# A graph layer on one core: the first gather of each part waits for ScalarE's work on the part three in front

## The chip, the cores and the metric

The kernel runs on one core of one Trainium2 chip. A core has a matrix engine (TensorE, written PE; its weight loads PEld), VectorE (DVE), ScalarE (ACT), GpSimd (POOL) and SyncE (SP, which here only issues transfers). Times are device microseconds (us) of one execution. The time before is the median of three runs.

## The reference

Nodes carry 128 features (`x`, 12,500 rows). There are 412,500 edges, sorted by their target node `dst`; each names a source node `src`.

```python
theta = x[dst] - x[src]
w = sigmoid(relu(theta @ W1 + b1) @ W2 + b2)
agg = segment_sum(w * theta, dst)
indeg = segment_sum(ones, dst)
y = x + agg + indeg * (x @ W4 + b4)
out = (y - mean(y)) / sqrt(var(y) + 1e-5)     # per row
```

## The kernel before

**Tables and parts.** The kernel first writes a table `z` to memory: for each node its row of `x @ W1` beside its row of `x`. The edges are then taken in 276 parts, numbered 0 to 275 (`s` in the code). Parts 0 to 17 are plain parts of 1,024 edges in the order given; parts 18 to 275 hold 1,532 edges each, of which 512 have one of the "hot" source nodes, whose rows TensorE makes from a table in on-chip memory (`tabs`), and at most 1,024 are gathered. Two parts make a block, which shares one sum in an accumulator.

**Gathers.** `gather(s)` issues eight indirect transfers from POOL (L401), each of 128 rows of 1 KB of `z`, into one of five buffers `zbuf` (`NZ = 5`); the last part has four. Part `s` uses the buffer of part `s - 5`. Since a gather overwrites a buffer, the framework makes it wait until its last readers are done: VectorE for the left half of the rows, ScalarE for the right half. It also waits for the landing of the gather eight before it (the counters `DMASW0` to `DMASW7`, one for each of the eight). POOL has next to nothing else to do in parts 18 to 275, and its gathers stand in the order of the parts.

**One part on the other engines.** `logits(s)` on VectorE subtracts the gathered rows from what TensorE spread over the edges (L951), applies the relu and the weights (L956), and sums (L962). ScalarE's `gate_sums` takes the sigmoid (L975), and `weigh_rest(s)` writes eight copies of the gathered rows, each weighted (L993, `wx`). L993 is the last reader of the part's buffer. TensorE adds the weighted copies up (L1158). Beside this VectorE works through `place()`, a long list of small steps that sorts the edges of the next 64 parts; `spend` hands them out by a credit per part. The sets of 64 begin at parts 18, 82, 146 and 210, and the gathers of a set need the indices that `place()` has made for it.

**What sets the order.** In the main loop (`part(s)`, for `s` from 18) the orders of TensorE, VectorE and ScalarE are as the code is written. POOL's gathers follow each other as they are issued. `gather` knows of a table `paced`: if the part is in it, the part's first gather gets one more wait, for the instruction noted there. In the kernel before, nothing is put into `paced`, so that the gathers are held back by the five buffers alone. `weighed[0]` always holds the newest weighted copy that was issued.

Gathers are issued four parts ahead in the early parts (`AHEAD = 4`) and three ahead in the main loop, from part 22 on, inside `spread_ahead`.

Of the kernel before, what the change touches and what calls it, by code (L numbers as in the profile page):

```python
# [37 lines left out]
AHEAD = 4  # L38
# [5 lines left out]
PLAIN = FIRST + MORE  # L44
# [40 lines left out]
def gnn_resnorm(  # L85
# [41 lines left out]
    NS = PLAIN - (E1 - E) // CE  # L127
# [32 lines left out]
    def set_of(s):  # L160

        s0 = 0 if s < PLAIN else PLAIN + (s - PLAIN) // S2 * S2
        return placed[s0], s - s0
# [8 lines left out]
    def load(i):  # L172

        s0, n, full = sets[i]
        es = ep.tile([P, WL], I32, name="es")
        ed = ep.tile([P, WL], I32, name="ed")
        bb = ep.tile([P, 1], I32, name="bb")
        dp = ep.tile([P, 1], I32, name="dp")
        e0 = E1 + (s0 - PLAIN) * CE
        if full < S2:  # L180
            nc.vector.memset(es, 0)
            for t in (ed, bb, dp):
                nc.vector.memset(t, N)
        for t, edges, m in ((es, src, HL), (ed, dst, WL)):
            for h in range(LISTS):
                nc.sync.dma_start(t[h * S2:h * S2 + full, :m], bass.AP(
                    tensor=edges.tensor, offset=edges.offset + e0 + h * HL, ap=[[CE, full], [1, m]]))
            if full < n:
                nc.sync.dma_start(
                    t[full:n, :TAIL], edges[E - TAIL:E].rearrange("(s e) -> s e", s=1))  # L190
        with nc.allow_non_contiguous_dma(reason="each block's and each part's first dst"):
            for h in range(LISTS):
                at = slice(h * S2, h * S2 + n)
                nc.sync.dma_start(bb[at], bass.AP(
                    tensor=dst.tensor, offset=dst.offset + e0, ap=[[SUB * CE, n // SUB], [0, SUB], [1, 1]]))
                nc.sync.dma_start(dp[at], bass.AP(
                    tensor=dst.tensor, offset=dst.offset + e0, ap=[[CE, n], [1, 1]]))
        return es, ed, bb, dp
# [172 lines left out]
    def slots(s):  # L371
        return [h * J + j for h in range(2) for j in range(pairs(s))]
# [7 lines left out]
    def wx_of(s):  # L380

        if s < NH:
            return wxe_buf[s % 2]
        return wx_buf[s % NW]

    def rows_of(s):

        if s < NH:
            t = zbuf[s // 2].rearrange("p k d -> p (k d)")[:, (s % 2) * BE:(s % 2 + 1) * BE]
            return t.rearrange("p (k d) -> p k d", d=D)  # L390
        return zbuf[(s - NH + NX) % NZ]
# [3 lines left out]
    paced = {}  # L395

    def gather(s):

        (src_i, _, _), i = set_of(s)
        for k in slots(s):  # L400
            ins = nc.gpsimd.indirect_dma_start(  # L401
                out=rows_of(s)[:, k, :], out_offset=None, in_=z if s >= NH else x,
                in_offset=IndirectOffsetOnAxis(ap=src_i[:, k, i:i + 1], axis=0))
            waits = [(gathers[-1], mybir.DependencyClass.NoSync)] if gathers else []
            at = (s * K + k) * 4 * len(chunks) // (NH * K) - 6
            if s < NH and 0 <= at < len(table_steps):
                waits.append((table_steps[at], mybir.DependencyClass.Sync))
            if k == 0 and s in paced:
                waits.append((paced[s], mybir.DependencyClass.Sync))
            for other, kind in waits:  # L410
                tc.add_manual_dep(
                    ins.ins, other.ins.name,
                    mybir.DependencyInfo(kind, mybir.DependencyReason.DATA), reason="gathers' pace")
            gathers.append(ins)
# [304 lines left out]
    with tc.manual_schedule(engines={SP}), tc.tile_pool(name="work", bufs=2) as wp, tc.tile_pool(  # L719
# [162 lines left out]
        def spread_y(s):  # L882

            d = parts[s]
            d["y"] = []
            for k0 in range(0, K if s < PLAIN else J, J):
                if s < NH:
                    spread_x(s, k0, copy_x(turn_x(s, k0)))
                    continue
                y = y_tile() if s < PLAIN - 1 else ps_y.tile([P, G, D], F32, name="y")  # L890
                d["y"].append(y)
                for j in range(J if s < PLAIN else pairs(s)):
                    nc.tensor.matmul(y[:, j, :], d["oh"][:, (k0 + j) * P:(k0 + j + 1) * P],  # L893
                                     y_of(s), start=True, stop=True)
# [94 lines left out]
        def weigh_rest(s):  # L989

            wx = wx_of(s)
            for k in slots(s):
                weighed[0] = nc.scalar.activation(wx[:, k, :D], rows_of(s)[:, k, D:], AF.Copy,  # L993
                                                  scale=wx[:, k, D:D + 1])
# [7 lines left out]
        weighed = [None]  # L1002
# [11 lines left out]
        def hot_load(f):  # L1014

            i0, g, i1, i = f
            a = i0
            while a < i1:
                (hot_s, _, n), j = hot_set(a)
                m = min(i1 - a, n - j)  # L1020
                nc.sync.dma_start(
                    hot_src[:, i % NU, (a - i0) * EP:(a - i0 + m) * EP],
                    hot_s[g, j:j + m].rearrange("(o p) l e -> o (p l e)", o=1).to_broadcast([P, m * EP]))
                a += m
# [77 lines left out]
        def hot_turned(t):  # L1102

            xT = xT_all[:, (t - PLAIN) % HX, :]
            nc.tensor.matmul(pz, wneg, xT, start=True, stop=False)  # L1105
            nc.tensor.matmul(pz, y_of(t), blocks[t // SUB]["oh"][:, BP:], start=False, stop=True)  # L1106

        def hot_relu(t):

            hr = parts[t]["hr"] = wp.tile([P, HK], F32, name="hr", bufs=1)  # L1110
            nc.scalar.activation(hr, pz, AF.Relu)  # L1111
# [169 lines left out]
        def fetch(b):  # L1281
            if b < NK:
                load_block(b)
# [48 lines left out]
        def tiles_of(group):  # L1332

            x = 0
            for f in group:
                hot_tiles(f, x)
                tiled.append((f, x))
                x += (f[2] - f[0]) * EP
# [19 lines left out]
        def fetch_step(s):  # L1358

            for f in rest_of:  # L1360
                if f[0] - 4 == s:
                    tiles_of([f])
# [125 lines left out]
        def spread_ahead(s):  # L1488

            if s + 2 < NS:  # L1490
                spread_y(s + 2)
                if PLAIN + AHEAD <= s + 3 < NS:
                    gather(s + 3)

        def part(s):

            b, h = divmod(s, SUB)
            t = s + 1
            credit[0] = min(credit[0] + 2.5, 5.0)
            if s in turns:  # L1500
                edges[s + 3] = turns[s], load(turns[s])
            if s in edges:
                i, loaded = edges.pop(s)
                assert steps[0] is None
                steps[:] = place(i, lambda: where[0](), *loaded), "k"
            for f in rest_of:
                if f[0] - 7 == s:
                    hot_load(f)
            if h == 0:
                fetch(b + 2)  # L1510
            if s == PLAIN:
                normalize(b - 2)
            done_b = h == 1 and PLAIN // SUB - 1 <= b - 1 < NK
            if t < NS:
                hot_turned(t)
            if t < NS:
                hot_relu(t)
            if done_b:
                total(b - 1)
            while opened:  # L1520
                hot_out(*opened.pop(0))
            advance("c")
            if s < NS:
                logits(s)
            if done_b:
                finish(b - 1)
            spread_ahead(s)
            if t < NS:
                hot_rows(t)
            sums = []  # L1530
            if h == 0 and PLAIN // SUB <= b - 1 < NK:
                sums = add_block(b - 1)
            if h == 1 and b < NK:
                sums = begin_block(b)
            issue(sums, products_of_tiles())
            if h == 0 and b + 1 < NK:
                one_hot(b + 1, BP, RW)
            if h == 1 and b + 2 < NK:
                one_hot(b + 2, 0, BP)
            if h == 1 and b < NK:  # L1540
                shift(b)
            if t < NS:
                hot_weights(t)
            if done_b:
                own(b - 1)
            if s < NS:
                if h == 0:
                    one_hot_h(b)
                gate_sums(s)
                weigh_rest(s)  # L1550
            fetch_step(s)
            spend("kxspmz")
            if done_b:
                normalize(b - 1)
# [204 lines left out]
```

## Time and profile before

| what | value |
|---|---|
| time, median of 3 runs | 2937.81 us (2935.55 to 2943.02) |
| the profiled execution's own time | 2943.8 us |
| its span, first to last instruction | 2942.0 us |
| busy: PE, PEld | 2548.2 us (87%), 2012.3 us (68%) |
| busy: DVE, ACT, POOL | 2380.3 us (81%), 2123.8 us (72%), 2164.5 us (74%) |
| gathers of parts 18 to 275 | 2060, 980 ns each in the mean |

A row of the timeline reads: start in us, duration in us, engine, line, operation, what is written `<-` what is read, how many instructions were merged, and in brackets how long the engine stood idle before it and what ended that. Rows of a source line begin with the line, the engine, the operation, the count, and the shortest, median and longest duration in ns. POOLq is POOL's sequencer. `zbuf<-z,src_i` as a DMA is a gather's landing. The first row of `zbuf<-z,src_i` is the first gather of part 18, so that a part's first gather is found by counting eights; in the same way the first L951 and the first eight L993 are those of part 18.

### The profile page before, as it was taken

What the parts mean: (1) busy time and instruction counts of PE and PEld (TensorE: products, weight loads), DVE (VectorE), ACT (ScalarE), POOL (GpSimd) and SP (SyncE); (2) the same over time, 40 slices, a digit from 0 to 9 for tenths busy, and PEclk for the clock granted to TensorE, in tenths of its full rate; (3) what the DMA queues carried; (4) which work ended last, traced back from release to release, by engine and by line L of the source; (5) the groups of instructions that cost most, each with busy time, mean ns of one, the idle gap of its engine ahead of it and who ended that gap; (6) DMA issues with size and microseconds to landing.
All of it is one profiled execution on the core that took longest, in us unless ns stands there. A gap on an engine that the chain in (4) does not pass through costs nothing.

```text
span 2942.0 us, 59129 instructions
## 1 busy us (share of the span) xinstructions
PE 2548.2 (87%) x18606; PEld 2012.3 (68%) x18606; DVE 2380.3 (81%) x4436; ACT 2123.8 (72%) x6416; POOL 2164.5 (74%) x2213
## 2 busy tenths in 40 slices
PE   6877899988888998998898888898998888888886
PEld 5656677777676777776776666676776666677764
DVE  7899699888957988888558888888568888888654
ACT  6365778767777777677777777776777777677776
POOL 4566777777777777777777777777777777777774
PEclk8688999989999999999999999999999999999998
DMA  8455555555554555554554545454554555555542
GB/s 285 151 153 123 142 139 138 140 135 137 140 146 134 137 140 140 133 141 135 143 150 133 135 133 141 132 141 134 143 142 128 140 132 141 133 138 141 141 134 77
DMA packets 239329, 413.58 MB, mean 141 GB/s; under 512 B 63423, under 2 KB 147226, under 8 KB 237470
## 3 DMA queue, kind: packets, MB, share of 16 engines
q0 software_dynamic: 105280, 286.93, 35.3%
q1 hardware_dynamic: 131756, 116.40, 15.3%
q10 hardware_dynamic: 1970, 6.40, 0.7%
q8 instruction: 148, 2.42, 0.3%
q14 instruction: 175, 1.43, 0.2%
HBM read 388.57 MB, written 20.94 MB: 139 GB/s over the span
## 4 chain that ended last, share of the span: by engine, by line
PE 38%; ACT 19%; DVE 15%; DMA 11%; issue 7%; POOL 1%; DVEq 0%; SPq 0%; ACTq 0%; POOLq 0%
PE pa L1158 14%; DMA zbuf<-z,src_i 10%; DVE zbuf L951 5%; PE y L893 5%; PE pd L1055 5%; ACT wx L993 5%; PE px L1119 4%; ACT wxh L1131 4%; PE pz L1105 3%; PE pz L1106 3%; PE pz L1122 3%; ACT oh L872 2%; ACT oh L873 2%; ACT xT L1069 1%; ACT a L1213 1%
## 5 line engine op out<-in xcount | busy, mean ns | idle before, releaser
L401 POOL DMA_INDIRECT zbuf<-z,src_i x2060 | 2018.5, 980 | 637.0 <-issue 236.6
L993 ACT ACTIVATE wx<-zbuf,wx 128x128 f32<-128x128 f32 x2060 | 630.2, 388 | 0.0
L1158 PE MATMUL pa<-wx,ow 128*104 128x260 f32 (+1 forms) x2284 | 628.4, 393 | 0.0
L893 PEld LDWEIGHTS y<-y,oh 128*128 128x128 f32 (+1 forms) x2156 | 276.1, 197 | 420.5 <-DVE zbuf L951 378.2
L1055 PEld LDWEIGHTS <-tabs 128*128 128x128 bf16 x6360 | 452.8, 101 | 124.2 <-issue 8.2
L951 DVE TENSOR_TENSOR zbuf<-y,zbuf 128x1024 f32<-128x1024 f32 x258 | 315.1, 1221 | 272.2 <-DMA zbuf<-z,src_i 270.9
L1055 PE MATMUL pd<-of,tabs 128*128 128x128 bf16 (+3 forms) x6360 | 535.2, 223 | 0.0
L1111 ACT ACTIVATE hr<-pz 128x512 f32<-128x512 f32 x258 | 152.9, 593 | 522.9 <-PE pz L1106 522.8
L893 PE MATMUL y<-y,oh 128*128 128x128 f32 (+1 forms) x2156 | 314.7, 291 | 228.7 <-DVE zbuf L951 220.6
L1158 PEld LDWEIGHTS pa<-wx,ow 128*104 128x104 f32 x2284 | 342.8, 179 | 40.6 <-issue 0.4
L962 DVE TENSOR_REDUCE lg<-zbuf 128x8 f32<-128x1024 f32 x273 | 329.8, 1208 | 13.2
L956 DVE SCALAR_TENSOR_TENSOR zbuf<-zbuf,fix 128x1024 f32<-128x1024 f32 x273 | 331.6, 1215 | 9.3
L1158 PE MATMUL pa<-wxh,owh 128*104 128x130 f32 x2064 | 329.0, 296 | 0.0
L1131 ACT ACTIVATE wxh<-pz,wxh 128x128 f32<-128x128 f32 x1032 | 295.2, 369 | 42.1 <-PE pz L1122 35.9
L1105 PE MATMUL pz<-xT,wni 128*128 128x512 f32 x516 | 278.5, 621 | 1.6 <-ACT wxh L1131 1.6
L1158 PEld LDWEIGHTS pa<-wxh,owh 128*104 128x104 f32 x2064 | 274.3, 186 | 0.0
L1119 PEld LDWEIGHTS px<-w_c,hr 128*128 128x128 f32 x2064 | 263.5, 200 | 7.8 <-ACT hr L1111 7.8
L1119 PE MATMUL px<-w_c,hr 128*128 128x1 f32 x2064 | 262.1, 248 | 5.6 <-ACT hr L1111 5.6
L1106 PE MATMUL pz<-oh,y 128*128 128x512 f32 x516 | 264.5, 594 | 0.1
L872 ACT ACTIVATE oh<-to_all,away,mine 128x512 f32<-128x512 bf16 (+1 forms) x257 | 213.6, 831 | 3.1 <-DMA to_all<-off_d 3.1
L1106 PEld LDWEIGHTS pz<-oh,y 128*128 128x128 f32 x516 | 98.2, 191 | 124.3 <-issue 123.4
L1122 PE MATMUL pz<-wni,xT 128*128 128x128 f32 x1032 | 176.3, 297 | 0.0
(304 smaller groups left out, 3595.8 us busy)
## 6 DMA issues: line engine op xcount, KB each, us to landing
to_all<-off_d SPq DMA_DIRECT2D x258, 128.0 KB
zbuf<-z,src_i POOLq DMA_INDIRECT x2060
hot_src<-hot_s SPq DMA_DIRECT2D x228, 128.0 KB
y<-z SPq DMA_DIRECT2D x270, 28.0 KB
xw<-in_x_dram SPq DMA_DIRECT2D x138, 52.0 KB
out_dram<-o SPq DMA_DIRECT2D x138, 52.0 KB
wx<-in_x_dram ACTq DMA_DIRECT2D x12, 512.0 KB
z<-zbuf SPq DMA_DIRECT2D x6, 1024.0 KB
```

What stands on the lines that cost most here:

```text
L401: ins = nc.gpsimd.indirect_dma_start(out=rows_of(s)[:, k, :], out_offset=None, in_=z if s >= NH else x, in_offset=IndirectOffsetOnAxis(ap= ...
L893: nc.tensor.matmul(y[:, j, :], d["oh"][:, (k0 + j) * P:(k0 + j + 1) * P], y_of(s), start=True, stop=True)
L951: nc.vector.tensor_sub(half, yy.to_broadcast([P, 2, n, D]), half)
L956: nc.vector.scalar_tensor_tensor(h[:, at, :], h[:, at, :], 0.0, w2.to_broadcast([P, n, D]), op0=OP.max, op1=OP.mult)
L962: nc.vector.tensor_reduce(lg[:, at, 0], h[:, at, :], AX.X, OP.add)
L993: weighed[0] = nc.scalar.activation(wx[:, k, :D], rows_of(s)[:, k, D:], AF.Copy, scale=wx[:, k, D:D + 1])
L1055: steps_of.append(lambda q=q, i=i, t=t, j=j: nc.tensor.matmul(to[:, q], tabs[:, g, i, q, t, :], of[:, t, q], start=j == 0, stop=j == HT * ...
L1105: nc.tensor.matmul(pz, wneg, xT, start=True, stop=False)
L1106: nc.tensor.matmul(pz, y_of(t), blocks[t // SUB]["oh"][:, BP:], start=False, stop=True)
L1119: nc.tensor.matmul(lgh()[:, t % SUB, q:q + 1], hr[:, at], w2_c, start=True, stop=True)
L1131: nc.scalar.activation(wx[:, q, :D], pz[:, q * P:(q + 1) * P], AF.Copy, scale=wx[:, q, D:D + 1])
L1158: return [lambda i=i, one=one, w=w: nc.tensor.matmul(to if len(w.shape) == 3 else to[:, 0, :], one, w, start=first and i == 0, stop=last a ...
```

## The change

Two lines leave `spread_ahead`, which stands in the first half of a part, and come back near the part's end, behind `weigh_rest(s)`. There the newest weighted copy, `weighed[0]`, is the eighth of part `s`; it is put into `paced[s + 3]` before `gather(s + 3)` is issued. So from part 22 on, the first of a part's eight gathers waits for the last weighted copy of the part three in front, besides the waits that it had.

```diff
@@ -1489,8 +1489,6 @@
             if s + 2 < NS:
                 spread_y(s + 2)
-                if PLAIN + AHEAD <= s + 3 < NS:
-                    gather(s + 3)
 
         def part(s):
@@ -1548,6 +1546,9 @@
                     one_hot_h(b)
                 gate_sums(s)
                 weigh_rest(s)
+            if PLAIN + AHEAD <= s + 3 < NS:
+                paced[s + 3] = weighed[0]
+                gather(s + 3)
             fetch_step(s)
             spend("kxspmz")
             if done_b:
```

On POOL, the last two gathers of part 25 and the eight of part 26 stand like this before. A row is one gather; the names with a number are the buffers and tables of this place, `Activation_49` and `DVE_49` are the counters of ScalarE and VectorE, and `DMASW` those of the landings. The value that is waited for is not shown.

```order
L401 DMA zbuf3_178<-z_60,src_i_2318 128x256 [waits DMASW6_49,Activation_49]
L401 DMA zbuf3_178<-z_60,src_i_2318 128x256 [waits DMASW7_49,Activation_49]
L401 DMA zbuf4_179<-z_60,src_i_2318 128x256 [waits DMASW0_49,DVE_49,Activation_49]
L401 DMA zbuf4_179<-z_60,src_i_2318 128x256 [waits DMASW1_49,Activation_49]
L401 DMA zbuf4_179<-z_60,src_i_2318 128x256 [waits DMASW2_49,Activation_49]
L401 DMA zbuf4_179<-z_60,src_i_2318 128x256 [waits DMASW3_49,Activation_49]
L401 DMA zbuf4_179<-z_60,src_i_2318 128x256 [waits DMASW4_49,Activation_49]
L401 DMA zbuf4_179<-z_60,src_i_2318 128x256 [waits DMASW5_49,Activation_49]
L401 DMA zbuf4_179<-z_60,src_i_2318 128x256 [waits DMASW6_49,Activation_49]
L401 DMA zbuf4_179<-z_60,src_i_2318 128x256 [waits DMASW7_49,Activation_49]
```

The same ten rows on POOL in the changed kernel:

```order
L401 DMA zbuf3_178<-z_60,src_i_2318 128x256 [waits DMASW6_49]
L401 DMA zbuf3_178<-z_60,src_i_2318 128x256 [waits DMASW7_49]
L401 DMA zbuf4_179<-z_60,src_i_2318 128x256 [waits DMASW0_49,DVE_49,Activation_49]
L401 DMA zbuf4_179<-z_60,src_i_2318 128x256 [waits DMASW1_49]
L401 DMA zbuf4_179<-z_60,src_i_2318 128x256 [waits DMASW2_49]
L401 DMA zbuf4_179<-z_60,src_i_2318 128x256 [waits DMASW3_49]
L401 DMA zbuf4_179<-z_60,src_i_2318 128x256 [waits DMASW4_49]
L401 DMA zbuf4_179<-z_60,src_i_2318 128x256 [waits DMASW5_49]
L401 DMA zbuf4_179<-z_60,src_i_2318 128x256 [waits DMASW6_49]
L401 DMA zbuf4_179<-z_60,src_i_2318 128x256 [waits DMASW7_49]
```

No gather has moved against another. The first of a part waits for a later value of ScalarE's counter, and the other seven no longer wait for ScalarE by themselves, since the first has done so for them.

The second place is POOL at the first part of the second set, part 82 (its table of indices is `src_i_8661`). Before:

```order
L401 DMA zbuf4_179<-z_60,src_i_2318 128x256 [waits DMASW6_49,Activation_49]
L401 DMA zbuf4_179<-z_60,src_i_2318 128x256 [waits DMASW7_49,Activation_49]
L401 DMA zbuf0_175<-z_60,src_i_8661 128x256 [waits DMASW0_49,DVE_49,Activation_49]
L401 DMA zbuf0_175<-z_60,src_i_8661 128x256 [waits DMASW1_49,Activation_49]
L401 DMA zbuf0_175<-z_60,src_i_8661 128x256 [waits DMASW2_49,Activation_49]
```

And in the changed kernel, on POOL:

```order
L401 DMA zbuf4_179<-z_60,src_i_2318 128x256 [waits DMASW6_49]
L401 DMA zbuf4_179<-z_60,src_i_2318 128x256 [waits DMASW7_49]
L401 DMA zbuf0_175<-z_60,src_i_8661 128x256 [waits DMASW0_49,DVE_49,Activation_49]
L401 DMA zbuf0_175<-z_60,src_i_8661 128x256 [waits DMASW1_49]
L401 DMA zbuf0_175<-z_60,src_i_8661 128x256 [waits DMASW2_49]
```

The new set's gathers follow the old set's at the same place of the row; only the waits differ. On TensorE, VectorE, ScalarE and SyncE every instruction stands where it stood, with the same kinds of waits.

## The prediction

> **What bounds the kernel now.** I read the page's busy shares first, then its groups, and then asked what POOL waits for.
>
> ```profile
> span 2942.0 us, 59129 instructions
> PE 2548.2 (87%) x18606; PEld 2012.3 (68%) x18606; DVE 2380.3 (81%) x4436; ACT 2123.8 (72%) x6416; POOL 2164.5 (74%) x2213
> L401 POOL DMA_INDIRECT zbuf<-z,src_i x2060 | 2018.5, 980 | 637.0 <-issue 236.6
> L951 DVE TENSOR_TENSOR zbuf<-y,zbuf 128x1024 f32<-128x1024 f32 x258 | 315.1, 1221 | 272.2 <-DMA zbuf<-z,src_i 270.9
> ```
>
> By busy shares TensorE leads and POOL comes fourth. But VectorE stands still 270.9 us for landings of gathers, and POOL's busy time leaves out what lies between two gathers. The waits of POOL from the first gather of part 22 to the end of part 274 (310.7 to 2910.7 us), and the gathers of that stretch:
>
> ```profile
> POOL zbuf L401 <- ACT wx L993: 142.7, 468, 0.3
> POOL zbuf L401 <- DMA zbuf<-z,src_i: 59.1, 194, 0.3
> ...
> L401 POOL DMA_INDIRECT zbuf<-z,src_i x2024: 942/949/1957, 310.7 to 2909.5; - x184
> ```
>
> The last number of a wait is its longest: 0.3 us, for every releaser. That is no wait but the step from one gather to the next. 2024 gathers in 2600 us make 1.285 us each; a median gather of 0.949 and the step of 0.305 make 1.254. So POOL issues without a pause for 2600 us, and the other 0.03 us per gather are gathers that last longer than the median. A part of eight takes at least 10.03 us and in the mean 2600 / 253 = 10.28. At the end the consumer waits for it:
>
> ```profile
> 2902.38 1.22 DVE L951 TENSOR_TENSOR zbuf<-y,zbuf 128x1024 f32<-128x1024 f32 x1 [5.07 <-DMA zbuf<-z,src_i]
> ```
>
> This is part 273, and VectorE stood still 5.07 us for its rows. Gather issue is the bound, and any pause that POOL takes after part 22 moves the end by its whole length, unless later gathers become shorter.
>
> **The added wait.** How soon a blocked gather starts once it is released is seen in the early parts, where a gather does wait for a weighted copy:
>
> ```profile
> 146.50 0.40 ACT L986 ACTIVATE wx<-zbuf,wx 128x128 f32<-128x128 f32 x1
> 147.17 1.35 POOL L401 DMA_INDIRECT zbuf<-z,src  x1 [7.06 <-ACT wx L986]
> ```
>
> The copy ends at 146.90, the gather starts at 147.17: 0.27 us. So each new start is the larger of the old one (with the delay gathered so far) and the end of part s-3's eighth copy plus 0.27. I compared all 254 parts so. First come the parts just behind part 22; the counts fix which rows they are (64 gathers from part 18 to 25, so that 351.65 is part 26; 40 copies of parts 18 to 22, so that 361.68 is part 23):
>
> ```profile
> L401 POOL DMA_INDIRECT zbuf<-z,src_i x64: 945/949/1611, 269.3 to 350.4; - x64
> 310.75 0.95 POOL L401 DMA_INDIRECT zbuf<-z,src_i  x1 [0.30 <-ACT xuT L820]
> 341.63 0.95 POOL L401 DMA_INDIRECT zbuf<-z,src_i  x1 [0.30 <-ACT px L550]
> 351.65 0.94 POOL L401 DMA_INDIRECT zbuf<-z,src_i  x1 [0.30 <-ACT wx L993]
> 362.75 0.95 POOL L401 DMA_INDIRECT zbuf<-z,src_i  x1 [0.30 <-ACT wx L993]
> ...
> L993 ACT ACTIVATE wx<-zbuf,wx x40: 385/387/402, 307.1 to 351.5; 128x128 f32<-128x128 f32 x40
> 314.98 2.45 ACT L993 ACTIVATE wx<-zbuf,wx 128x128 f32<-128x128 f32 x8
> 349.41 2.45 ACT L993 ACTIVATE wx<-zbuf,wx 128x128 f32<-128x128 f32 x8
> 361.68 2.45 ACT L993 ACTIVATE wx<-zbuf,wx 128x128 f32<-128x128 f32 x8
> 369.32 2.45 ACT L993 ACTIVATE wx<-zbuf,wx 128x128 f32<-128x128 f32 x8
> ```
>
> - Part 22 started at 310.75; part 19's copies end at 314.98 + 2.45 = 317.43. New start 317.70: delay 6.95.
> - Part 25: 341.63 + 6.95 = 348.58 against 349.41 + 2.45 + 0.27 = 352.13. Delay 10.50.
> - Part 26: 351.65 + 10.50 = 362.15 against 361.68 + 2.45 + 0.27 = 364.40. Delay 12.75.
> - Part 27: 362.75 + 12.75 = 375.50, and part 24's copies end at 371.77: no further wait. Nor is there one at 23 and 24, or for 50 parts from here.
>
> Does this delay reach the end? The consumer lags here, so the rows lie ready for long:
>
> ```profile
> 383.00 1.22 DVE L951 TENSOR_TENSOR zbuf<-y,zbuf 128x1024 f32<-128x1024 f32 x1
> 501.45 1.23 DVE L951 TENSOR_TENSOR zbuf<-y,zbuf 128x1024 f32<-128x1024 f32 x1
> 520.76 1.22 DVE L951 TENSOR_TENSOR zbuf<-y,zbuf 128x1024 f32<-128x1024 f32 x1 [0.58 <-DMA zbuf<-z,src_i]
> 487.74 0.94 POOL L401 DMA_INDIRECT zbuf<-z,src_i  x1 [0.30 <-issue]
> ```
>
> VectorE begins part 26 at 383.00, 20 us after its last gather was issued (part 27's first starts at 362.75), and part 39 at 501.45: 118.45 / 13 = 9.11 us per part. POOL goes from part 26's first gather at 351.65 to part 39's at 487.74: 10.47 per part. The consumer gains about 1.36 us per part, and by part 41 (520.76) it already waits for a landing in the kernel before. The 20 us of lead are thus spent in any case. With 12.75 gone at part 26, the meeting comes about ten parts sooner, and from there everything runs 12.75 later. The lead covers the pause when it happens and not at the end. What is queued behind the waiting gather is POOL's every later gather, and behind these VectorE's L951.
>
> The next place is the second set's start, where `place()` crowds VectorE and the copies come late again (512 gathers make parts 18 to 81, so that 930.58 is part 82; 488 copies make parts 18 to 78, so that 930.54 is part 79):
>
> ```profile
> L401 POOL DMA_INDIRECT zbuf<-z,src_i x512: 942/949/1957, 269.3 to 929.1; - x171
> 930.58 1.16 POOL L401 DMA_INDIRECT zbuf<-z,src_i  x1 [0.30 <-ACT wx L975]
> L993 ACT ACTIVATE wx<-zbuf,wx x488: 384/387/404, 307.1 to 919.4; 128x128 f32<-128x128 f32 x163
> 930.54 2.44 ACT L993 ACTIVATE wx<-zbuf,wx 128x128 f32<-128x128 f32 x8
> 891.47 1.22 DVE L951 TENSOR_TENSOR zbuf<-y,zbuf 128x1024 f32<-128x1024 f32 x1 [1.64 <-DMA zbuf<-z,src_i]
> ```
>
> 932.98 + 0.27 - 930.58 = 2.67 us. Part 77 (891.47) still waited for its rows, so that consumer and gathers enter this place equally late, and the whole 2.67 is added.
>
> Elsewhere the copies are in time. The smallest margin is at part 196 (2102.02), against part 193; a usual one is part 140 (1524.56), against part 137:
>
> ```profile
> 2099.08 2.45 ACT L993 ACTIVATE wx<-zbuf,wx 128x128 f32<-128x128 f32 x8
> 2102.02 0.95 POOL L401 DMA_INDIRECT zbuf<-z,src_i  x1 [0.30 <-ACT hr L1111]
> 1512.91 2.44 ACT L993 ACTIVATE wx<-zbuf,wx 128x128 f32<-128x128 f32 x8
> 1524.56 0.95 POOL L401 DMA_INDIRECT zbuf<-z,src_i  x1 [0.30 <-ACT wx L993]
> ```
>
> 2102.02 - 2101.53 - 0.27 = 0.22 us to spare at part 196, and 8.94 at part 140. Near 196 one pause of up to 2.67 (the size seen at part 82) could appear if copies come later; I take 0 and keep 2.67 for the range.
>
> **The removed waits.** Parts 22 to 274 lose seven waits for ScalarE each, and the last part three: 253 x 7 + 3 = 1774. Such a wait is a sequencer instruction of 17 ns. The kernel's first gathers show the step without one:
>
> ```profile
> 7.75 0.95 POOL L401 DMA_INDIRECT zbuf<-in_x_dram,src  x1 [0.30 <-issue]
> 9.01 0.95 POOL L401 DMA_INDIRECT zbuf<-in_x_dram,src  x1 [0.30 <-issue]
> L401 POOLq EVENT_SEMAPHORE  x1: 17/17/17, 12.1 to 12.1; - x1
> ```
>
> Up to 12.1 us there is no such instruction, and the step is the same 0.30. It runs while the gather before it is busy, so I price it at nothing; bounds 0 and 1774 x 17 ns = 30.2 us gained. These gathers, with no such wait at all, stand for the first. The other engines' instructions keep their places and cost nothing new: SP's queue is not passed by anything, and POOL's holds only gathers.
>
> **Gathers that last longer.** The pause lies over 341 to 364 us, where gathers run beside VectorE's `place()` steps:
>
> ```profile
> 310.70:508.10 197.40, 151.08 (x152) 0.97 0.51 137
> 360.76 1.68 POOL L401 DMA_INDIRECT zbuf<-z,src_i  x1 [0.30 <-issue]
> 361.54 0.55 DVE L566 TENSOR_SCALAR ed<-ed 128x767 int32<-128x767 int32 x1
> ```
>
> 152 gathers of parts 22 to 40 were busy 151.08 us, where 152 x 0.949 = 144.2: 6.9 us longer than at the median. If the pause falls on the moments at which gathers are stretched, up to 6.9 us come back; if the later start meets more of them, as much may be lost. I take 0. [...]
>
> **The sum.** 12.75 + 2.67 = 15.42 us on the profiled execution: 2943.8 + 15.4 = 2959.2. That execution stands 6.0 above the median of 2937.81; the change is added to the median: 2953.2 us, 0.52% slower.
>
> **The rivals.**
> - *Faster: shorter steps.* If the 17 ns of each dropped wait do count, 30.2 us are gained against 15.4 lost: 2937.8 + 15.4 - 30.2 = 2923.0. It would decide the sign from 8.7 ns per wait on. Against it stands the unchanged 0.30 step above.
> - *No change: the lead absorbs the pause.* With 20 us of rows ready at part 26, 12.75 could be hidden, leaving at most 2.67: 2938 to 2940.5. It needs a consumer that stays behind POOL to the end; the waits at 520.76 and 2902.38 speak against it.
> - *Little change: the pause spares stretched gathers.* 15.4 - 6.9 = 8.5: 2946.3. [...] But gathers that start later have other steps beside them.
> - *More pauses.* Set starts at 146 and 210 and the tight place at 196 could each add up to 2.67, which makes up to 8 us: 2961.2.
> - *A pause in every part.* If the copies came 9 us later against the gathers than now, POOL would stop in nearly all 254 parts; one us each makes 2937.8 + 254 = 3192. The 8.94 us of part 140 speak against it.
>
> **How the numbers follow.** Within 0.3% (8.8 us) is about what a measurement of this kernel cannot tell from no change. Chances: the forecast 0.62, more pauses 0.14, spared gathers 0.10, absorbed 0.07, shorter steps 0.04, a pause in every part 0.03. Spared gathers end just inside the bound; of their chance 0.03 is counted beyond it and 0.07 within. Slower: 0.62 + 0.14 + 0.03 + 0.03 = 0.82; within: 0.07 + 0.07 = 0.14; faster 0.04. The range runs from the spared case less 2 us of scatter between runs (their lowest is 2.3 below the median), 2944, to the paused case with the same, 2963; this holds 0.86 by the chances.
>
> **What would show it.** POOL's waits for L993 would have a longest of about 7 us instead of 0.3, with three pauses by part 26 (6.95, 3.55, 2.25) and about 2.7 at parts 81 and 82, and no other above 0.3. Between them the step stays 0.30 and a pair of gathers 1.254. VectorE would first wait for a landing near part 31 instead of part 41, and the end would still be a wait for gathers. The prediction is wrong if steps become shorter, if pauses appear in the regular parts, or if the gathers' mean of 980 ns changes by more than 3 ns (6 us over 2024).

## The result and the profile after

The changed kernel takes 2955.03 us (median of 5 runs, 2954.05 to 2963.86) against 2939.18 for the kernel before (5 runs, 2935.55 to 2943.02): 15.85 us more. The ratio is 1.0063, with a 95% interval of 1.0044 to 1.0083. The forecast was 2953.2, 15.4 us more.

In ten of the twelve experiment runs TensorE was granted only 0.76 to 0.83 of its clock (0.936 in the profiles of the other two, 0.937 and 0.935 in those of before and after), and the kernel before took 4043 to 4148 us beside them instead of 2940, so that those runs have a section of their own.

The page of the changed kernel, in the lines that answer to those of before:

```profile
span 2952.1 us, 57355 instructions
PE 2560.8 (87%) x18606; PEld 2023.6 (69%) x18606; DVE 2381.8 (81%) x4436; ACT 2124.4 (72%) x6416; POOL 2160.8 (73%) x2213
L401 POOL DMA_INDIRECT zbuf<-z,src_i x2060 | 2015.2, 978 | 651.1 <-issue 533.4
L951 DVE TENSOR_TENSOR zbuf<-y,zbuf 128x1024 f32<-128x1024 f32 x258 | 315.2, 1222 | 294.2 <-DMA zbuf<-z,src_i 292.5
```

59129 - 57355 = 1774 instructions are gone, which are the dropped waits. POOL's idle time before gathers went from 637.0 to 651.1. VectorE waits 21.6 us longer for landings. The waits of POOL from part 22's first gather on; the last number of a row is its longest wait:

```profile
POOL zbuf L401 <- issue: 528.2, 1734, 0.3
POOL zbuf L401 <- ACT wx L993: 49.3, 114, 7.9
POOL zbuf L401 <- DVE zbuf L951: 11.6, 38, 0.3
```

ScalarE's weighted copy is now the one releaser behind which POOL stands for longer than a step. There are four such places in 254 parts. The first gathers of parts 22, 25, 26 and 210, each behind the copies that released it:

```profile
315.81 2.45 ACT L993 ACTIVATE wx<-zbuf,wx 128x128 f32<-128x128 f32 x8
318.53 0.94 POOL L401 DMA_INDIRECT zbuf<-z,src_i  x1 [7.89 <-ACT wx L993]
...
350.24 2.45 ACT L993 ACTIVATE wx<-zbuf,wx 128x128 f32<-128x128 f32 x8
352.96 0.94 POOL L401 DMA_INDIRECT zbuf<-z,src_i  x1 [4.05 <-ACT wx L993]
...
363.43 2.45 ACT L993 ACTIVATE wx<-zbuf,wx 128x128 f32<-128x128 f32 x8
366.14 0.94 POOL L401 DMA_INDIRECT zbuf<-z,src_i  x1 [2.05 <-ACT wx L993]
...
2254.80 2.45 ACT L993 ACTIVATE wx<-zbuf,wx 128x128 f32<-128x128 f32 x8
2257.51 0.94 POOL L401 DMA_INDIRECT zbuf<-z,src_i  x1 [1.85 <-ACT wx L993]
```

Each gather starts 0.26 or 0.27 us behind the end of the copies. Without the ordinary step of 0.305 the pauses are 7.58, 3.74, 1.74 and 1.55: 14.6 us.

The two profiled spans differ by 10.1 us only. The 2060 gathers together were 3.3 us shorter (2018.5 to 2015.2), which takes 14.6 to 11.3, and most of the remaining 1.2 lies behind the last gather: from its end to the end of the span it is 25.2 us, where it was 26.6. The shorter gathers are not put down to the change. The median is 946 ns where it was 949, but one kernel, run three times below, had 949, 949 and 946; and with four in front (below) the median is 946 too and the total 2020.3.

### The profile page after: what moved, and what is told of

Same layout as the page of the kernel before. It is cut to its first block, busy times and chain, and to the rows that moved or that the text cites. A ratio compares the mean times of both kernels' runs of the same rounds, so it can differ in the third digit from the quotient of the medians.

```text
span 2952.1 us, 57355 instructions
## 1 busy us (share of the span) xinstructions
PE 2560.8 (87%) x18606; PEld 2023.6 (69%) x18606; DVE 2381.8 (81%) x4436; ACT 2124.4 (72%) x6416; POOL 2160.8 (73%) x2213
## 4 chain that ended last, share of the span: by engine, by line
PE 29%; ACT 15%; POOL 14%; DVE 14%; issue 10%; DMA 9%; DVEq 0%; ACTq 0%; SPq 0%; POOLq 0%
POOL zbuf L401 14%; PE pa L1158 11%; DMA zbuf<-z,src_i 8%; DVE zbuf L951 5%; PE y L893 4%; PE pd L1055 4%; ACT wx L993 3%; PE px L1119 3%; ACT wxh L1131 3%; PE pz L1105 2%; PE pz L1106 2%; PE pz L1122 2%; ACT oh L872 2%; ACT oh L873 1%; ACT xT L1069 1%
## 5 line engine op out<-in xcount | busy, mean ns | idle before, releaser
L401 POOL DMA_INDIRECT zbuf<-z,src_i x2060 | 2015.2, 978 | 651.1 <-issue 533.4
L993 ACT ACTIVATE wx<-zbuf,wx 128x128 f32<-128x128 f32 x2060 | 630.3, 388 | 0.0
```

Of the source, the lines that this page charges most:

```text
L401: ins = nc.gpsimd.indirect_dma_start(out=rows_of(s)[:, k, :], out_offset=None, in_=z if s >= NH else x, in_offset=IndirectOffsetOnAxis(ap= ...
```

## The experiments with the clock granted

**The change once more.** No edit; the question was how far the pauses repeat.

> The changed kernel once more, with a profile of its own. Its five times so far lie in two groups, three at 2954 to 2955 and two at 2963 to 2964. If gathers bound the kernel and pauses add up, a profile of the fast group shows 13 us of pauses by part 26 and 0 to 3 later, and one of the slower group 8 us more of pauses at set starts (parts 82, 146, 210). Where the chip halves TensorE's clock for much of the time (granted clock near 0.8), the other kernels with this wait took 17 us for a part against 14 to 15 without it: there the change would cost 10% or more.

2958.46 us (4 runs) against 2942.62: 1.0057, interval 1.0037 to 1.0076. Its profiled execution took 2958.18 us. The pauses at parts 22, 25 and 26 come back (gaps of 7.87, 4.04 and 3.05 us), and two set starts show one each, part 146 and part 210:

```profile
1603.12 0.95 POOL L401 DMA_INDIRECT zbuf<-z,src_i  x1 [1.52 <-ACT wx L993]
...
2262.43 0.94 POOL L401 DMA_INDIRECT zbuf<-z,src_i  x1 [1.58 <-ACT wx L993]
```

Without the steps that is 14.05 + 2.49 = 16.5 us. The three pauses behind part 22 came in both profiles; which set starts are late differs between them, by a few us. Three of the nine times are 2963 to 2966 us, and no profile was taken of such an execution, so their extra 8 us are not explained.

**Four in front instead of three.** The same place in the code and the same seven dropped waits per part, but the release comes one part earlier:

```diff
     paced = {}
+    lasts = {}
...
             if PLAIN + AHEAD <= s + 3 < NS:
-                paced[s + 3] = weighed[0]
+                paced[s + 3] = lasts[s - 1]
                 gather(s + 3)
+            lasts[s] = weighed[0]
```

> The same kernel as the change but for the release: the first gather waits for the last copy of the part four in front. If TensorE's clock is granted and the loss is POOL's pauses: one pause of 0.5 to 3 us by part 27, none later, and within 0.1% of before, 14 to 17 us faster than the change. If the loss came from the gathers' new place in the program or from the dropped waits: as slow as the change (0.6%). If dropped waits shorten the step: 6 to 30 us faster than before. If the clock is halved for much of the time: 13 to 17% slower, as twice before.

2945.77 us (12 runs) against 2940.49 (17 runs): 1.0012, interval 1.0002 to 1.0021. Its page, its POOL waits, and the only two gaps above a step (one line more in the code moves every line number by one):

```profile
span 2947.3 us, 57355 instructions
...
L402 POOL DMA_INDIRECT zbuf<-z,src_i x2060 | 2020.3, 981 | 638.3 <-issue 535.6
```

```profile
POOL zbuf L402 <- issue: 530.4, 1741, 0.3
POOL zbuf L402 <- ACT wx L994: 41.7, 131, 1.6
```

```profile
354.06 0.94 POOL L402 DMA_INDIRECT zbuf<-z,src_i  x1 [0.81 <-ACT wx L994]
...
366.58 0.94 POOL L402 DMA_INDIRECT zbuf<-z,src_i  x1 [1.58 <-ACT wx L994]
```

The instruction count is that of the change to the last one, so place and dropped waits are the same. The pauses are 0.81 + 1.58 - 0.61 = 1.8 us in place of 14.6 to 16.5, which is 12.8 to 14.7 less. The loss falls from 0.57 to 0.63% to 0.12%: by 0.45 to 0.51%, or 13 to 15 us. So the release time of three parts carries the loss; neither the gathers' new place in the program nor the dropped waits do. Nor did the dropped waits gain: with 1774 fewer the kernel is not faster than before. Two details were expected otherwise: two parts are held, 26 and 27, and not one, and the 0.12% lie just outside "within 0.1%".

## The experiments under a halved clock

These were meant to split the loss by place and to test its size, and do not, since gather issue is not the bound in them: with the wait up to part 40, for one, POOL itself stands still for L993, up to 31.5 us at a time, and VectorE waits 0.8 us in all for landings:

```profile
POOL zbuf L401 <- ACT wx L993: 1272.7, 399, 31.5
DVE zbuf L951 <- DMA zbuf<-z,src_i: 0.8, 4, 0.2
```

They show something else. The two kernels that put the wait on some parts alone are the change with one condition, here for parts 22 to 40; the other kernel has `s + 3 >= 41` in its place:

```diff
             if PLAIN + AHEAD <= s + 3 < NS:
-                paced[s + 3] = weighed[0]
+                if s + 3 < 41:
+                    paced[s + 3] = weighed[0]
                 gather(s + 3)
```

Expected of the wait for parts 22 to 40, which was run three times:

> The new wait for parts 22 to 40 alone; from part 41 on gathers are held by the five buffers as before. If each pause of POOL behind part 22 reaches the end, this alone costs 12.75 us by the rows of before (three pauses at parts 22, 25, 26) or 13.1 by those seen in the changed kernel: 0.44% slower, with no pause after part 26. If the consumer's lead absorbs the pause, it costs 0 to 2 us. If dropped waits shorten the step, the few dropped here (19 parts x 7) give nothing that can be seen.

> The new wait for parts 22 to 40 alone, on a chip that grants TensorE nearly its full clock (0.93 or more), where gathers bound the kernel. If each pause of POOL behind part 22 reaches the end: 12.75 us by the rows of before, 13.1 by those of the changed kernel, 0.44% slower, with no pause after part 26. If the consumer's lead absorbs it: 0 to 2 us. If the chip halves the clock for much of the time again (granted clock near 0.8), TensorE bounds the kernel and neither theory is tested.

> The new wait for parts 22 to 40 alone, third attempt to have it with TensorE's clock granted. If pauses behind part 22 reach the end: the profile shows three pauses of 13 to 14 us in all by part 26 as the changed kernel does, none later, and the time is 0.44 to 0.48% (13 to 14 us) over before; the 2 to 3 us that the change costs beyond this come from the set starts. If the lead absorbs them: 0 to 2 us. If dropped waits in the regular parts matter, the steps here are those of before and the time differs from the changed kernel's by more than 5 us.

Expected of the wait from part 41 on, which was run twice:

> The new wait from part 41 on alone. If pauses add up, this costs only what the set starts do: 1.5 us (the one pause that the changed kernel's profile shows, at part 210) to 2.7 (the pause that was forecast at part 82), at most 8 with a pause at each of three set starts; 0.05 to 0.27% slower. If the loss came from the regular parts after all, this costs most of the 16 to 18 us. If the 1700 or so dropped waits shorten the steps, it is 3 us or more faster.

> The new wait from part 41 on alone, with the clock granted. If pauses add up: what the set starts cost, 1.5 us (the pause at part 210 in the changed kernel's profile) to 2.7 (forecast at part 82), at most 8; 0.05 to 0.27% slower. If the loss came from the regular parts: most of 16 to 18 us. If some 1700 dropped waits shorten the steps: 3 us or more faster.

Four in front, as above, twice:

> Same place in the code and the same dropped waits, but the first gather waits for the last copy of the part four in front. By the rows of before this comes one part (about 10 us) earlier everywhere, and only part 26 or 27 is held, by 0.5 to 1.7 us. If pauses add up and the dropped waits cost and gain nothing: within 0.1% of before. If the dropped waits shorten the step (3 ns each as a first look at the changed kernel might suggest, 17 ns at most): 6 to 30 us faster. If moving the gathers in the program costs something by itself: slower by what it costs.

> The first gather waits for the last copy of the part four in front, with the clock granted. Same place in the code and the same 1774 dropped waits as in the change, but the release comes about 10 us earlier. If pauses add up and dropped waits cost and gain nothing: within 0.1% of before (0.5 to 1.7 us of pause at part 26 or 27). If dropped waits shorten the step: 6 to 30 us faster. If moving the gathers in the program costs something by itself: slower by that.

Two in front is the change with an index moved:

```diff
-            if PLAIN + AHEAD <= s + 3 < NS:
-                paced[s + 3] = weighed[0]
-                gather(s + 3)
+            if PLAIN + AHEAD <= s + 2 < NS:
+                paced[s + 2] = weighed[0]
+                gather(s + 2)
```

> The first gather waits for the last copy of the part two in front. The usual margin of 8.94 us at three in front is less than a part's 10.28, so that POOL now stops in more than half of all parts. By the rows of before, replayed with this wait: about 35 us by part 41, and some 300 us in all (10% slower). If a pause is absorbed by the consumer's lead wherever it falls: far less, 40 us or so.

One pause alone is the kernel before, with parts 26 and 27 taken out of `spread_ahead` and issued behind `weigh_rest(24)`:

```diff
-                if PLAIN + AHEAD <= s + 3 < NS:
+                if PLAIN + AHEAD <= s + 3 < NS and s + 3 not in (26, 27):
                     gather(s + 3)
...
                 weigh_rest(s)
+            if s == 24:
+                paced[26] = weighed[0]
+                gather(26)
+                gather(27)
```

> Only part 26 waits, for the last copy of part 24 (two in front); all other gathers are as before. By the rows of before the pause is 369.32 + 2.45 + 0.27 - 351.65 = 20.4 us, as long as the whole lead that VectorE leaves there (20 us). If any pause behind part 22 reaches the end: 20 us slower, 0.69%, in one piece. If a pause is absorbed by the lead: 0 to 2 us.

> Only part 26 waits, for the last copy of part 24; every other gather and every other wait is as before. With TensorE's clock granted: if any pause behind part 22 reaches the end, one pause of 20 to 21 us (20.4 by the rows of before, longer by what this chip is later there) and 0.69% slower, though the pause is about as long as the lead of rows that VectorE has at that place. If the lead absorbs it: 0 to 2 us. If the clock is halved for much of the time: TensorE is the bound and the result tells nothing of this.

Measured, each against the kernel before, which was run beside it:

| kernel | us | before, us | ratio (95% interval) | clock in its profile |
|---|---|---|---|---|
| wait for parts 22 to 40 | 4153.4 | 4111.7 | 1.0078 (1.0047 to 1.0108) | 0.808 |
| same, again | 4117.4 | 4043.5 | 1.0179 (1.0115 to 1.0244) | 0.819 |
| same, a third time | 4154.7 | 4122.8 | 1.0108 (1.0021 to 1.0196) | 0.807 |
| wait from part 41 | 4578.7 | 4111.7 | 1.113 (1.109 to 1.117) | 0.764 |
| same, again | 4667.2 | 4043.5 | 1.157 (1.152 to 1.163) | 0.765 |
| four in front | 4644.9 | 4111.7 | 1.131 (1.126 to 1.135) | 0.762 |
| same, again | 4716.2 | 4043.5 | 1.171 (1.165 to 1.176) | 0.758 |
| two in front | 4647.1 | 4111.7 | 1.128 (1.122 to 1.133) | 0.763 |
| one pause at part 26 | 4071.9 | 4043.5 | 1.0078 (1.0038 to 1.0118) | 0.827 |
| same, again | 4154.2 | 4147.5 | 1.0054 (1.0010 to 1.0098) | 0.812 |

The expectations that supposed gathers to be the bound missed by far with four in front, which costs 13 to 17% where it cost 0.12% with the clock granted, and with the wait from part 41 on. Two in front was priced at 300 us by pauses and took 535 us more, as much as four in front (533). The first two runs of the wait up to part 40 lie above the expected 0.44%. For one pause at part 26, and for the third run of the wait up to part 40, the expected 0.69% and 0.44 to 0.48% lie inside the measured intervals. That is no test of them, since gathers were not the bound there: the pause itself was 44 us long and not 20.4. VectorE's waits for landings with the wait from part 41 on, and with two in front:

```profile
DVE zbuf L951 <- DMA zbuf<-z,src_i: 0.5, 2, 0.3
```

```profile
DVE zbuf L951 <- DMA zbuf<-z,src_i: 544.6, 123, 8.1
```

With the wait from part 41 VectorE waits for landings 0.5 us in all, and with two in front 544.6 us, at the same time within 2%. So late gathers are not what costs with the wait from part 41; for two in front these numbers leave it open. Busy time and granted clock by stretch, for the wait up to part 40 (parts to 40 lie in the first stretch) and then for the wait from part 41 (parts from 41 lie in the other two); the columns are PE, PEld, DVE, ACT, POOL, clock, DMA share and GB/s:

```profile
400.00:680.00 280.00, 190.81 (x1083) 129.72 (x1084) 143.90 (x262) 124.37 (x381) 126.15 (x131) 0.75 0.30 82
800.00:1200.00 400.00, 304.12 (x1964) 230.98 (x1964) 248.78 (x461) 220.88 (x679) 221.46 (x230) 0.85 0.37 102
```

```profile
400.00:650.00 250.00, 178.51 (x1078) 133.57 (x1079) 138.17 (x254) 126.28 (x384) 122.70 (x127) 0.77 0.32 88
800.00:1200.00 400.00, 270.50 (x1557) 180.72 (x1558) 208.45 (x397) 173.69 (x543) 172.64 (x183) 0.75 0.30 80
2000.00:3000.00 1000.00, 680.68 (x4036) 471.75 (x4034) 492.50 (x878) 454.92 (x1413) 457.53 (x480) 0.76 0.31 85
```

Early and late stretches of one kernel differ in their work, so the two kernels are compared stretch by stretch. In the first, POOL issues 131 gathers in 280 us with the wait, 17.1 us per part of eight, and 127 in 250 us without it, 15.7. From 800 to 1200 us it issues 183 with the wait, 17.5 us per part, and 230 without it, 13.9. In both the kernel with the wait is the slower one, and its TensorE has the lower clock (0.75 against 0.77, and 0.75 against 0.85). Where the time is lost is seen in TensorE's group of small products. In the kernel before, with the clock granted, TensorE has no idle time ahead of it; with four in front it has 495.9 us, and somewhat more ahead of the sums of the weighted copies (L1159). The last three rows show one cycle of the stall by stretches of the time; their columns are PE's busy time, clock, DMA share and GB/s:

```profile
L1055 PE MATMUL pd<-of,tabs 128*128 128x128 bf16 (+3 forms) x6360 | 535.2, 223 | 0.0
```

```profile
L1056 PE MATMUL pd<-of,tabs 128*128 128x128 bf16 (+3 forms) x6360 | 651.3, 228 | 495.9 <-issue 493.2
L1159 PE MATMUL pa<-wx,ow 128*104 128x260 f32 (+1 forms) x2284 | 887.3, 468 | 586.1 <-issue 572.6
```

```profile
1993.30:2006.90 13.60, 13.16 (x115) 1.00 0.19 59
2006.90:2010.40 3.50, 0.60 (x5) 1.00 0.75 190
2010.40:2027.40 17.00, 8.37 (x17) 0.50 0.27 79
```

TensorE first nearly stops for 3.5 us at a full clock, waiting for nothing that the profile shows, and the clock is halved only then. The order is the same at all 143 falls of the clock behind 400 us in this profile: in the 3 us ahead of a fall TensorE was busy 26% of the time in the mean, against 67% in the 10 us ahead. So in this profile each fall comes behind a stall; that the stall brings the fall about is the author's inference from this order, and no run tests it.

The stall goes with the transfers. In four in front behind 400 us, while the clock is full, TensorE stands without a visible wait 4% of the time when the DMA engines are less than 20% busy, and 37% when they are over 80% busy (counted in steps of half a microsecond); in the second row above the DMA share is 0.75. With the clock granted, in four profiles, such standing makes less than 1 us in all, whatever the DMA share. This is a coincidence in time and not yet a cause. What stalls TensorE, and why the wait on a part's first gather makes it worse, stays open: gathers, the copies and the clock repeat together, so that these runs cannot part them (the cycle above lasts 34.1 us, and POOL issues 480 gathers there from 2000 to 3000 us, which makes 33.3 us for two parts). It is no fixed property of a chip: one chip took 4716 us for four in front and later 2946 for the same kernel, and one of the twelve executions behind that 2946 took 3474.7 us at a granted clock of 0.646.

Not settled with the clock granted are therefore three things that were planned: the loss of parts 22 to 40 by itself, a pause as long as the whole lead, and two in front.

## Why the prediction was right, step by step

- **Gather issue is the bound.** Held. Between the pauses the step stays at 0.30 us, and the delay stays to the end: part 26's first gather starts 14.5 us later than before (366.14 and 351.65), and part 273's rows are taken 11.5 us later (2913.90 and 2902.38), the gathers being some 3 us shorter. There VectorE still waits, 5.02 us.

```profile
2913.90 1.23 DVE L951 TENSOR_TENSOR zbuf<-y,zbuf 128x1024 f32<-128x1024 f32 x1 [5.02 <-DMA zbuf<-z,src_i]
```

- **The pauses behind part 22.** Forecast 6.95, 3.55 and 2.25 us, 12.75 in all; measured 7.58, 3.74 and 1.74, 13.1 in all, and 14.05 in the second profile. The parts were the right ones, and so was the 0.27 us between the copies' end and the start. The largest pause lies at 310 to 318 us, though, and not "over 341 to 364 us".
- **The lead covers the pause only for a while.** Held. Part 26 began on VectorE at 384.68, part 31 at 432.38 with a wait of 2.32, as was said ("near part 31 instead of part 41"). By part 41 VectorE takes its rows some 15 us later than before, about as late as the gathers are:

```profile
384.68 1.23 DVE L951 TENSOR_TENSOR zbuf<-y,zbuf 128x1024 f32<-128x1024 f32 x1
...
432.38 1.22 DVE L951 TENSOR_TENSOR zbuf<-y,zbuf 128x1024 f32<-128x1024 f32 x1 [2.32 <-DMA zbuf<-z,src_i]
```

- **2.67 us at part 82.** Wrong in place, and near in size by luck. No pause came there; part 210 took 1.55 in one profile, parts 146 and 210 together 2.5 in the other. The step that failed is "consumer and gathers enter this place equally late". In the profile after, VectorE takes part 77's rows 13.0 us later than before (904.43 and 891.47), as was supposed, and stands still 4.72 us for them. But ScalarE's next step in that part, which had waited 3.09 us for TensorE before and does so again, comes only 10.1 us later, so that part 79's copies are 9.8 us later, the gathers 13.3, and the copies end in time. The first row is of before:

```profile
894.82 0.60 ACT L1111 ACTIVATE hr<-pz 128x512 f32<-128x512 f32 x1 [3.09 <-PE pz L1106]
...
904.43 1.23 DVE L951 TENSOR_TENSOR zbuf<-y,zbuf 128x1024 f32<-128x1024 f32 x1 [4.72 <-DMA zbuf<-z,src_i]
904.89 0.60 ACT L1111 ACTIVATE hr<-pz 128x512 f32<-128x512 f32 x1 [3.09 <-PE pz L1106]
940.36 2.45 ACT L993 ACTIVATE wx<-zbuf,wx 128x128 f32<-128x128 f32 x8
943.89 0.95 POOL L401 DMA_INDIRECT zbuf<-z,src_i  x1 [0.30 <-ACT xT L1069]
```

So ScalarE hung on TensorE there and not on the gathers, and VectorE's wait of 1.64 us showed only that VectorE was as late as the gathers. The second profile repeats this: copies 9.2 us later, gathers 14.0. A margin read from a single execution is also good to some 3 us only: at part 196 it is 0.22 us before, 3.59 in the first profile of the change and 0.22 in the second. The other two set starts had 0.83 (part 146) and 0.76 us (part 210) to spare before, well within that. The rival "more pauses" does not show in the two profiles: set starts took 1.55 and 2.5 us in all, less than the 2.67 that the sum held for them.
- **Dropped waits cost and gain nothing.** Held: four in front drops the same 1774 and is 0.12% slower than before, not faster. The lower end of its interval, 0.6 us slower, with 1.8 us of pauses, leaves 1.2 us for a gain, where the rival had 30.2.
- **Stretched gathers: 0.** Held within 2 us for parts 22 to 40, and within 3 us for all 2028 gathers from part 22 on, of which 226 lasted over 30 ns longer than the median before and 227 after, by 63.5 and 66.2 us together. The rival that the pause spares them fell. The gathers of parts 22 to 40 were busy for

```profile
318.40:522.50 204.10, 152.28 (x152) 0.94 0.49 132
```

```profile
362.41 1.68 POOL L401 DMA_INDIRECT zbuf<-z,src_i  x1 [0.30 <-issue]
363.19 0.55 DVE L566 TENSOR_SCALAR ed<-ed 128x767 int32<-128x767 int32 x1
```

152.28 us against 152 x 0.946 = 143.8, or 8.5 us longer, where it had been 6.9. The 1.68 us gather stands beside L566 again, though it is another part's gather now: later gathers met the same VectorE steps. What lengthens a gather there is not shown, nor how many gathers a shifted order will stretch.
- **The sum.** Forecast 15.4 us, measured 15.85 and 15.84 us in two comparisons of medians. That the agreement is within half a microsecond is luck. The pauses are 14.6 us in one profile and 16.5 in the other, the times of the changed kernel spread over 12 us, and the two profiled executions of before and after differ by 10.25 us only.

## What to carry to other kernels

Where one engine issues without a pause from some point to the end, a wait put ahead of it costs about its whole length (here 14.6 and 16.5 us of pauses, and 15.85 us of time), even if the consumers have 20 us of work in stock at that moment, as here, since the stock runs out before the end and the lost issue time does not come back. To price such a wait, line up every start of the bound engine with the end of what it would wait for, and add up the overshoots: here three places in the first 5% of the gathers made most of the pauses (13.1 of 14.6 us, and 14.05 of 16.5), while the usual part had 9 us to spare. Margins below the scatter between executions (3 us here) should go into the range, not into the sum, and not at a fixed place. And a wait of one engine of the consumer does not show that the others are as late: ask which engine sets the time of what the new wait waits for.

## What the runs showed of the hardware that was not expected

- The kernel before ran at 4043 and at 2940 us on one chip, within the same hour. With four in front at a granted clock of 0.762, TensorE stalls without a visible wait, 493.2 us ahead of one group of products alone, and the granted clock falls to one half behind such stalls, in stretches whose median is 17 us.
- There one wait ahead of a part's first gather cost 11 to 17% against the kernel before, whose eight gathers wait for their buffer each by itself; with the clock granted, four in front and the kernel before differ by 0.12%.
- A gather's median length is 949 ns in some runs and 946 in others of the same kernel, here for the wait up to part 40 in its first run and its third:

```profile
L401 POOL DMA_INDIRECT zbuf<-z,src_i x1099: 941/949/1774, 799.3 to 2788.4; - x184
```

```profile
L401 POOL DMA_INDIRECT zbuf<-z,src_i x1083: 940/946/1637, 799.7 to 2796.3; - x181
```

Over 2060 gathers 3 ns are 6 us, more than the smaller term of the sum. Two profiles should be compared by their pauses and counts before their spans.
